# Opening the recurrence's buffers before layer 1's attention

## The chip, the cores and the metric

The kernel runs on one core of one Trainium2 chip. A core has five engines that work in parallel, each through its own list of instructions in order: TensorE (PE: matrix products, and transposes by a product with the identity), VectorE (DVE), ScalarE (ACT), GpSimd (POOL) and SyncE (SP, which here only issues DMAs). They wait for one another through semaphores. Data lies in SBUF (128 partitions), products in PSUM banks. The metric is the device time of one execution in microseconds. The kernel before the change takes 1873.88 us, the median of three runs (1872.47 to 1874.83).

## The reference

Two layers work on x, 3327 rows of 256 features, and on a symmetric 0/1 adjacency matrix. Layer 0 is a graph attention with two heads, followed by a mixture of 16 experts. Layer 1 is a graph attention with one head, followed by a recurrence of 30 steps on the normalized rows. The change lies in layer 1, where this is computed:

```python
# graph attention of layer 1, on h = layernorm(x)
wh = h @ W
e = wh @ a[:256] + (wh @ a[256:]).T
e = where(e > 0, e, 0.2 * e)
e = where(adj > 0, e, -9e15)
x = x + elu(softmax(e, axis=-1) @ wh)

# recurrence of layer 1, on h = layernorm(x); 30 times
h = h + 0.01 * tanh(h)
h = h * sigmoid(h)
h = layernorm(h, ln_w, ln_b)
h = h @ W.T + b

x = x + h
```

## The kernel before, in words

The rows are cut into 26 tiles of 128, which stay in SBUF as `x` the whole time. Everything is computed in float32.

Layer 1's attention (`attend`, L202) goes over nine parts of three target tiles each (`groups2`; the last part has two). In each part it goes over the 26 source tiles. For a source tile, ACT writes `e` (a Relu, L276), DVE makes the masked weights `pT` from `e`, the row `part` and the adjacency `adjT` (L281), and PE adds three products with `s_wh` to three accumulators in PSUM (L286; each product is two matmul instructions in the profile). `e` and `pT` have three buffers each (pool `edge2`). When a part is done, its accumulators are closed while the next part is already running: for each tile, DVE takes a reciprocal and the two halves of the elu from the accumulator (L257, L999, L1000), ACT an exponential (L1001), and DVE adds the result to `x` (L1002, L1003). `begin_state` (L1005) then stores the rows of `x` to DRAM as `kept` and normalizes them in place (statistics on DVE at L116 to L119, a power on POOL at L121, L128 on DVE). So `x` holds the recurrence's starting state, scaled by S = 100, for one part after another while the attention is still running.

The recurrence works on seven groups of four tiles (the last has two), 30 steps, so 210 groups in all, numbered through by `at`. A group goes through these steps, each a method of `Group`: `tanh` (ACT, L1046), `add` (POOL, L1049), `silu` (ACT, L1053), `measure` (DVE, L1058 and L1061), `invert` (POOL, L1066 and L1067), then a transposition of z, `product` (PE, L1101, with PSUM tile `po`) and `evict` (DVE, L1111, which writes the new `x`). The transposition has two forms. `turn_here` uses PE, eight transposes into two PSUM banks (L1077), and ACT copies these to `zT` (L1079). `turn_away`, for groups 1, 3 and 5 of every step, lets ACT split z into 16-bit halves (L1086), writes them to DRAM by a DMA of SP (L1087), and reads them back by a transposing DMA of SP (L1091). The loop at the end staggers the groups: in the pass `at`, the product of group `at` stands beside the tanh of group `at + 6` and the add of group `at + 5`.

A scheduler orders the instructions of each engine, from the dependencies and its own idea of durations; `tc.keep_in_program_order` takes an instruction out of its hands. The recurrence pins all its instructions from the second step on (`put`, L1041); in the first step it pins only PE's products and transposes.

Buffers come from pools. A pool that is opened after others were closed takes their memory, and its first writers wait for those that used it last. The names the change touches:

- `steps` (L944): two buffers each of `th`, `z` and `zT`, opened ahead of layer 1's attention. `add_results` (L956) uses them at the layer's start to load the experts' results (L962); in the recurrence `turn_here` takes its `zT`, and `turn_away` its `th` and `z`.
- `wide` (L1025): four buffers each of `wth` and `wz`, which hold the recurrence's tanh and silu. It is opened after the attention's pools (`keep2`, `work2`, `edge2`, `rows2`, `fin2`) are closed, and lies in their memory.
- `narrow` (L1026): the small statistics of the recurrence, opened at the same place.
- `ps` (two PSUM banks, opened ahead of the attention), `ps_t` and `ps_o`, opened after it. `turn_here` takes its banks from `ps` and `ps_t` in turn.

Of the kernel before, what the change touches and what calls it, by code (L numbers as in the profile page):

```python
# [11 lines left out]
F32 = mybir.dt.float32  # L12
I32 = mybir.dt.int32
I16 = mybir.dt.int16
# [7 lines left out]
P = 128  # L22
# [4 lines left out]
G = 4  # L27
# [4 lines left out]
def gat_moe_gat_recurrent_ffn(ctx: ExitStack, tc: tile.TileContext, a: dict, out: bass.AP):  # L32
    nc = tc.nc
    N, D = a["x"].shape
    KD = D // P
# [88 lines left out]
    def normalized(src, dst, scale=1.0):  # L124

        r, mv, power = inverse(src, scale)
        for j in range(len(src)):
            nc.vector.tensor_scalar(  # L128
                dst[j], src[j], mv[:, j, 0:1], r[:, j : j + 1], op0=ALU.subtract, op1=ALU.mult
            )  # L130
        return power

    def without_mean(wv, n_out, ones, p):

        for k in range(KD):
            nc.tensor.matmul(p[:, :n_out], lhsT=ones, rhs=wv[:, k, :], start=(k == 0), stop=(k == KD - 1))
        for k in range(KD):
            nc.vector.scalar_tensor_tensor(
                wv[:, k, :], p[:, :n_out], -1.0 / D, wv[:, k, :], op0=ALU.mult, op1=ALU.add
            )  # L140
# [43 lines left out]
    class Scores:  # L184


        def __init__(self, pool, heads, s=None):
            self.s = pool.tile([P, NT, 2, heads], F32, name="s") if s is None else s
            self.row = pool.tile([P, NT, heads], F32, name="row")
            self.full = pool.tile([P, NT, heads], F32, name="full")  # L190
            self.part = pool.tile([P, NT, heads], F32, name="part")
            self.minus = pool.tile([P, NT, heads], F32, name="minus")
# [189 lines left out]
    with ExitStack() as moe:  # L382
# [267 lines left out]
        two = rec.tile([P, 2, SLOTS], F32, name="prod")  # L650
# [290 lines left out]


    kept = dram.tile([NP, D], F32, name="kept")
    steps = ctx.enter_context(tc.tile_pool(name="steps", bufs=2))  # L944
    ps = ctx.enter_context(tc.tile_pool(name="ps2", bufs=2, space=PSUM))
    with ExitStack() as st:
        keep = st.enter_context(tc.tile_pool(name="keep2", bufs=1))

        s_wh = keep.tile([P, NT, 1, D + 3], F32, name="s_wh")
        wh = s_wh[:, :, :, 2:]  # L950
        sc = Scores(keep, 1, s_wh[:, :, 0, 0:2].rearrange("p t (s h) -> p t s h", h=1))
        work = st.enter_context(tc.tile_pool(name="work2", bufs=2))
        ps_o = st.enter_context(tc.tile_pool(name="ps2o", bufs=2, space=PSUM))
        names = cycle(("th", "z", "zT"))

        def add_results(some):  # L956
            for ts in some:
                n, two = len(ts), []
                for k in range(2):
                    here = slice(k * NP + ts[0] * P, k * NP + (ts[-1] + 1) * P)  # L960
                    two.append(steps.tile([P, G, D], F32, name=next(names))[:, :n, :])
                    nc.sync.dma_start(two[k], given[here, :].rearrange("(t p) d -> p t d", p=P))  # L962
                here = x[:, ts[0] : ts[-1] + 1, :]
                for k in range(2):
                    nc.vector.tensor_tensor(here, here, two[k], ALU.add)


        without_mean(wv1, D + 2, ones_r, ps.tile([P, 512], F32, name="bank"))
        recurrence_parameters(lambda: ps.tile([P, 512], F32, name="bank"))
        add_results(groups1[:3])  # L970
        tc.keep_in_program_order(nc.vector.memset(wh[:, :, :, D : D + 1], 1.0))
        count = 1

        def spot():
            nonlocal count
            count += 1
            return ps_o.tile([P, 512], F32, name=f"acc{count % 3}")

        def split1(t, p, r):
            nc.scalar.activation(s_wh[:, t, 0, : D + 2], p[:, : D + 2], AF.Copy, scale=r)  # L980
            for ts in groups1:
                if t == ts[-1]:
                    sc.finish(ts[0], t + 1)

        project(
            groups1, wv1, D + 2, split1, work, ps, spot,
            lambda ts, power: add_results(groups1[groups1.index(ts) + 3 :][:1]),
        )
        nc.vector.tensor_scalar(wh[:, NT - 1], wh[:, NT - 1], real[:, 0:1], None, op0=ALU.mult)

        run = st.enter_context(tc.tile_pool(name="edge2", bufs=3))
        rows_p = st.enter_context(tc.tile_pool(name="rows2", bufs=2))
        fin = st.enter_context(tc.tile_pool(name="fin2", bufs=2))

        def add_elu(t, pr, h, po, r):

            low = fin.tile([P, D], F32, name="low")
            high = fin.tile([P, D], F32, name="high")
            nc.vector.tensor_scalar(low[:pr], po, r, 0.0, op0=ALU.mult, op1=ALU.min)  # L999
            nc.vector.tensor_scalar(high[:pr], po, r, 0.0, op0=ALU.mult, op1=ALU.max)  # L1000
            nc.scalar.activation(low[:pr], low[:pr], AF.Exp)  # L1001
            nc.vector.scalar_tensor_tensor(high[:pr], low[:pr], -1.0, high[:pr], op0=ALU.add, op1=ALU.add)  # L1002
            nc.vector.tensor_tensor(x[:pr, t, :], x[:pr, t, :], high[:pr], ALU.add)  # L1003

        def begin_state(ts):  # L1005
            here = slice(ts[0] * P, (ts[-1] + 1) * P)
            nc.sync.dma_start(kept[here, :].rearrange("(t p) d -> p t d", p=P), x[:, ts[0] : ts[-1] + 1, :])
            yield
            tiles = [x[:, t, :] for t in ts]
            normalized(tiles, tiles, S)  # L1010

        attend(
            sc, wh, 1, groups2, 1, add_elu, begin_state, (run, rows_p, ps, ps_o), deque(),
            (nc.sync, 1, lambda: fin.tile([P, D], F32, name="low")),
        )


    with ExitStack() as st:
# [3 lines left out]
        last_p = st.enter_context(tc.tile_pool(name="last", bufs=2))  # L1022

        apart = [dram.tile([G * P, 2, D], I16, name=f"apart{q}") for q in range(2)]
        wide = st.enter_context(tc.tile_pool(name="wide", bufs=4))  # L1025
        narrow = st.enter_context(tc.tile_pool(name="narrow", bufs=8))  # L1026

        AWAY = (1, 3, 5)
        COUNT = len(groups)
        LAST = N_STEPS * COUNT  # L1030

        class Group:

            def __init__(self, at):
                self.at = at
                self.ts = groups[at % COUNT]
                self.n = len(self.ts)
                self.hs = x[:, self.ts[0] : self.ts[0] + self.n, :]
                self.away = at % COUNT in AWAY

            def put(self, ins):  # L1041
                return tc.keep_in_program_order(ins) if self.at >= COUNT else ins

            def tanh(self):
                self.th = wide.tile([P, G, D], F32, name="wth")[:, : self.n, :]
                self.put(nc.scalar.activation(self.th, self.hs, AF.Tanh, scale=1.0 / S))  # L1046

            def add(self):
                self.put(nc.gpsimd.tensor_tensor(self.th, self.th, self.hs, ALU.add))  # L1049

            def silu(self):
                self.z = wide.tile([P, G, D], F32, name="wz")[:, : self.n, :]
                self.put(nc.scalar.activation(self.z, self.th, AF.Silu, scale=1.0 / S))  # L1053

            def measure(self):
# [12 lines left out]

            def turn_here(self):
                pool = next(turns)  # L1070
                zT = steps.tile([P, G, KD, P], F32, name="zT")
                for c in range(self.n // 2):
                    pt = pool.tile([P, 2, KD, P], F32, name="bank")
                    for j in range(2):
                        for k in range(KD):
                            tc.keep_in_program_order(
                                nc.tensor.transpose(pt[:, j, k, :], self.z[:, 2 * c + j, k * P : (k + 1) * P], ident)  # L1077
                            )
                    self.put(nc.scalar.copy(zT[:, 2 * c : 2 * c + 2, :, :], pt))  # L1079
                self.zT = lambda j, k: zT[:, j, k, :]  # L1080

            def turn_away(self):
                n = self.n
                parts = steps.tile([P, G, 2, D], I16, name="th")[:, :n]
                here = apart[self.at % COUNT // 2 % 2][: n * P]
                self.put(nc.scalar.copy(parts, self.z.bitcast(I16).rearrange("p j (d b) -> p j b d", b=2)))  # L1086
                nc.sync.dma_start(  # L1087
                    here.rearrange("(j p) b d -> p j (b d)", p=P), parts.rearrange("p j b d -> p j (b d)")
                )
                zT = steps.tile([P, KD, G * P], F32, name="z")  # L1090
                nc.sync.dma_start(  # L1091
                    zT.bitcast(I16)[:, :, : n * 2 * P], here.rearrange("t b d -> (t b) d"), transpose=True
                )
                self.zT = lambda j, k: zT[:, k, j * P : (j + 1) * P]
# [98 lines left out]
```

## Time and profile before

| | |
|---|---|
| median of three runs | 1873.88 us (1872.47 to 1874.83) |
| the profiled execution: its time / its span | 1875.77 us / 1874.0 us |
| granted TensorE clock, mean of the span | 0.992 |
| PE busy | 1815.3 us, 97% of the span |
| DVE / ACT / POOL busy | 1281.8 / 1177.1 / 936.9 us |
| layer 1's attention, first to last product | 784.2 to 1080.9 us |
| first tanh of the recurrence | 1080.93 us |
| product of the second step's first group | 1124.74 us |
| one settled step | 25.5 us |

PE, DVE, ACT and POOL are named as above; SPq is SP's list of DMA issues, PEld the loading of weights, which runs beside PE. Times in the timeline count from the start of the span. In brackets stands how long the engine sat idle before an instruction and what ended that idle time. A number such as L1046 is a line of the kernel before; in the changed kernel the same line stands four or five lines further down.

### The profile page before, as it was taken

To read this page: it belongs to the slowest core of one execution; us is meant where nothing else is said; L and a number is where in the kernel's file an instruction comes from. 1 tells how busy PE (TensorE), PEld (TensorE's weight loads), DVE (VectorE), ACT (ScalarE), POOL (GpSimd) and SP (SyncE) were. 2 spreads that over 40 slices of the span, in tenths; PEclk is the share of its full clock that TensorE was granted. 3 is DMA by queue.
4 is the path that set the end of the run, shared out by engine and by line. 5 is a ranking of instruction groups with operands and counts; after the bars stand their busy time and mean duration, and the time that the engine had idled before them with its cause. 6 is when DMAs were issued, how large, how long until landed. Compare 5 with 4: busy or idle time off the path is not lost.

```text
span 1874.0 us, 32159 instructions
## 1 busy us (share of the span) xinstructions
PE 1815.3 (97%) x11204; PEld 1658.8 (89%) x11204; DVE 1281.8 (68%) x3829; ACT 1177.1 (63%) x1487; POOL 936.9 (50%) x864
## 2 busy tenths in 40 slices
PE   6999999999999998999999979999999999999997
PEld 6999999998999997788888868888888888888886
DVE  6888888842222222666767678888888888888887
ACT  2877777631111111655555578888888888888884
POOL 3010212255333331100000079999999999999994
PEclk9999999999999999999999989999999999999999
DMA  8887260179999885300000045545554555554556
GB/s 175 113 126 96 53 99 23 59 237 300 344 336 338 298 273 183 106 13 18 22 13 17 16 110 133 124 127 122 124 124 124 124 127 122 125 122 124 124 130 197
DMA packets 379919, 255.04 MB, mean 136 GB/s; under 512 B 240917, under 2 KB 339532, under 8 KB 379754
## 3 DMA queue, kind: packets, MB, share of 16 engines
q1 hardware_dynamic: 363634, 220.08, 43.0%
q0 software_dynamic: 11440, 28.09, 8.6%
q10 hardware_dynamic: 4680, 4.76, 0.8%
q8 instruction: 92, 1.51, 0.3%
q14 instruction: 73, 0.60, 0.1%
HBM read 168.19 MB, written 77.01 MB: 131 GB/s over the span
## 4 chain that ended last, share of the span: by engine, by line
PE 67%; issue 10%; POOL 6%; DVE 5%; DMA 4%; ACT 1%; SPq 0%; POOLq 0%; DVEq 0%; ACTq 0%
PE po L1101 34%; PE acc L286 25%; PE bank L1077 5%; POOL given L855 2%; POOL rb L761 2%; DVE pT L281 2%; DMA given<-wh,to 2%; DMA old<-kept 1%; DMA wh<-in_w_dram 1%; PE bank L835 1%; POOL wth L1049 1%; PE acc L163 1%; PE bank L526 1%; PE bank L148 0%; DMA lists<-pair,ati 0%
## 5 line engine op out<-in xcount | busy, mean ns | idle before, releaser
L276 ACT ACTIVATE e<-rb,minus,full 128x384 f32<-128x384 f32 (+3 forms) x494 | 402.4, 824 | 189.2 <-DVE pT L281 172.4
L1049 POOL TENSOR_TENSOR wth<-wth,x 128x1024 f32<-128x1024 f32 (+1 forms) x210 | 464.8, 2214 | 17.2 <-ACT wth L1046 17.2
L281 DVE SCALAR_TENSOR_TENSOR pT<-e,part,adjT 128x384 f32<-128x384 f32 (+3 forms) x494 | 374.7, 761 | 135.8 <-PE acc L286 120.4
L1111 DVE SCALAR_TENSOR_TENSOR x<-po,rr,bb 128x256 f32<-128x256 f32 x780 | 322.9, 475 | 99.4 <-PE po L1101 63.3
L1101 PE MATMUL po<-wc,zT 128*128 128x256 f32 x1680 | 384.2, 380 | 3.2 <-DVE x L1111 3.2
L1101 PEld LDWEIGHTS po<-wc,zT 128*128 128x128 f32 x1680 | 313.4, 191 | 43.1 <-ACT wz L1053 2.2
L1101 PE MATMUL po<-wc,z 128*128 128x256 f32 x1440 | 325.6, 379 | 0.0
L286 PE MATMUL acc<-wh,pT 128*128 128x129 f32 x2704 | 309.8, 276 | 2.1 <-DVE pT L281 2.1
L286 PEld LDWEIGHTS acc<-wh,pT 128*128 128x128 f32 x2704 | 305.0, 192 | 2.7 <-DVE pT L281 2.5
L1101 PEld LDWEIGHTS po<-wc,z 128*128 128x128 f32 x1440 | 271.3, 190 | 35.7
L286 PE MATMUL acc<-s_wh,pT 128*128 128x257 f32 x1352 | 295.8, 382 | 2.4 <-DVE pT L281 2.4
L286 PEld LDWEIGHTS acc<-s_wh,pT 128*128 128x128 f32 x1352 | 257.6, 191 | 40.4 <-DVE pT L281 3.8
L1058 DVE BATCH_NORM_STATS2 stats<-wz 128x6 f32<-128x256 f32 x780 | 274.4, 413 | 27.5 <-ACT wz L1053 27.3
L1053 ACT ACTIVATE wz<-wth 128x1024 f32<-128x1024 f32 (+1 forms) x210 | 208.0, 990 | 82.7 <-POOL wth L1049 82.4
L121 POOL TENSOR_TENSOR rstd<-ve,neg_half 128x4 f32<-128x4 f32 (+3 forms) x28 | 30.4, 1087 | 441.4 <-DVE ve L119 290.4
L1046 ACT ACTIVATE wth<-x 128x1024 f32<-128x1024 f32 (+1 forms) x210 | 209.8, 999 | 26.7 <-DVE x L1111 22.7
L1067 POOL TENSOR_TENSOR rr<-rr,neg_half 128x4 f32<-128x4 f32 (+1 forms) x210 | 208.2, 992 | 17.5
L1086 ACT COPY th<-wz 128x2048 int16<-128x2048 int16 x90 | 170.9, 1899 | 1.8
L881 ACT ACTIVATE e<-bank 128x512 f32<-128x512 f32 x61 | 36.4, 597 | 196.2 <-PE bank L835 188.8
L885 DVE TENSOR_TENSOR pT<-e,bank 128x512 f32<-128x512 f32 x61 | 41.9, 687 | 166.8 <-PE bank L835 166.7
L835 PEld LDWEIGHTS bank<-hT,wh 128*128 128x128 f32 x1280 | 149.3, 192 | 5.2 <-ACT hT L827 1.4
L835 PE MATMUL bank<-hT,wh 128*128 128x128 f32 x1280 | 150.5, 275 | 2.6 <-DMA wh<-in_w_dram 2.6
(195 smaller groups left out, 1636.3 us busy)
## 6 DMA issues: line engine op xcount, KB each, us to landing
wh<-in_w_dram SPq DMA_DIRECT2D x120, 512.0 KB
apart<-th SPq DMA_DIRECT2D x90, 512.0 KB
first_set<-in_w_dram SPq DMA_DIRECT2D x63, 512.0 KB
in_bytes<-in_adj_dram POOLq DMA_DIRECT2D x3, 2496.0 KB, 28.3
x<-in_x_dram SPq DMA_DIRECT2D x6, 512.0 KB
kept<-x SPq DMA_DIRECT2D x8, 384.0 KB
old<-kept SPq DMA_DIRECT2D x6, 512.0 KB
out_dram<-x SPq DMA_DIRECT2D x6, 512.0 KB
```

The lines of the kernel that those rows point to most:

```text
L276: nc.scalar.activation(e[:, : n * P], rb[:, : n * P], AF.Relu, scale=sc.full[:, j, h : h + 1], bias=sc.minus[:, j, h : h + 1],)
L281: masked = nc.vector.scalar_tensor_tensor(pT[:, : n * P], e[:, : n * P], sc.part[:, j, h : h + 1], adjT[:, j // 2, ts[0] * P : (ts[-1] + 1 ...
L286: nc.tensor.matmul(po[c], lhsT=pT[:, c * P : (c + 1) * P], rhs=wh[:, j, h, :], start=(j == 0 and c % per_bank == 0), stop=(j == NT - 1), s ...
L835: nc.tensor.matmul(p[:, f, :], lhsT=w[:, k, f * P : (f + 1) * P], rhs=hT[:, k, :], start=(k == 0), stop=(k == KD - 1),)
L1046: self.put(nc.scalar.activation(self.th, self.hs, AF.Tanh, scale=1.0 / S))
L1049: self.put(nc.gpsimd.tensor_tensor(self.th, self.th, self.hs, ALU.add))
L1053: self.put(nc.scalar.activation(self.z, self.th, AF.Silu, scale=1.0 / S))
L1058: self.put(nc.vector.bn_stats(stats[:, j, :], self.z[:, j, :]))
L1067: self.put(nc.gpsimd.tensor_tensor(r, r, neg_half[:, : self.n], ALU.pow))
L1086: self.put(nc.scalar.copy(parts, self.z.bitcast(I16).rearrange("p j (d b) -> p j b d", b=2)))
L1101: nc.tensor.matmul(self.po[:, j, :], lhsT=self.zT(j, k), rhs=wc[:, k, :], start=(k == 0), stop=(k == KD - 1),)
L1111: nc.vector.scalar_tensor_tensor(self.hs[:, j, :], self.po[:, j, :], self.r[:, j : j + 1], bb, op0=ALU.mult, op1=ALU.add)
```

## The change

The buffers of the recurrence's tanh and silu (now `th` with three buffers and `z` with four) move to the pools that are opened ahead of layer 1's attention, and so do the statistics (`narrow`). `add_results` uses the same pools as before, now with 3, 4 and 2 buffers. `turn_away` gets a pool of its own, `apart`, opened where `wide` was. In the first step, group 1 is turned by PE instead of through DRAM (`and at > 1`), and the transposes of groups 0 and 1 are no longer pinned.

```diff
-    steps = ctx.enter_context(tc.tile_pool(name="steps", bufs=2))
+    steps = {
+        name: ctx.enter_context(tc.tile_pool(name=f"steps_{name}", bufs=bufs))
+        for name, bufs in (("th", 3), ("z", 4), ("zT", 2))
+    }
+    narrow = ctx.enter_context(tc.tile_pool(name="narrow", bufs=8))
...
-                    two.append(steps.tile([P, G, D], F32, name=next(names))[:, :n, :])
+                    name = next(names)
+                    two.append(steps[name].tile([P, G, D], F32, name=name)[:, :n, :])
...
-        wide = st.enter_context(tc.tile_pool(name="wide", bufs=4))
-        narrow = st.enter_context(tc.tile_pool(name="narrow", bufs=8))
+        apart_p = st.enter_context(tc.tile_pool(name="apart", bufs=2))
...
-                self.away = at % COUNT in AWAY
+                self.away = at % COUNT in AWAY and at > 1
...
-                self.th = wide.tile([P, G, D], F32, name="wth")[:, : self.n, :]
+                self.th = steps["th"].tile([P, G, D], F32, name="th")[:, : self.n, :]
...
-                self.z = wide.tile([P, G, D], F32, name="wz")[:, : self.n, :]
+                self.z = steps["z"].tile([P, G, D], F32, name="z")[:, : self.n, :]
...
-                zT = steps.tile([P, G, KD, P], F32, name="zT")
+                zT = steps["zT"].tile([P, G, KD, P], F32, name="zT")
...
-                            tc.keep_in_program_order(
+                            (tc.keep_in_program_order if self.at > 1 else lambda ins: ins)(
...
-                parts = steps.tile([P, G, 2, D], I16, name="th")[:, :n]
+                parts = apart_p.tile([P, G, 2, D], I16, name="parts")[:, :n]
...
-                zT = steps.tile([P, KD, G * P], F32, name="z")
+                zT = apart_p.tile([P, KD, G * P], F32, name="zTa")
```

## The prediction

> **What bounds the kernel now.** I read the page first: the chain that ended last is 67% PE, and its largest line, L1101 (the recurrence's products), fills the whole second half. Then the table of busy time by stage (columns: stretch, its length, then busy time and instruction count of PE, PEld, DVE, ACT and POOL, granted clock, DMA share, GB/s):
>
> ```profile
> 784.20:1055.30 271.10, 271.10 (x1243) 237.22 (x1244) 172.25 (x383) 153.91 (x231) 5.96 (x7) 0.99 0.05 17
> 1055.30:1080.90 25.60, 24.63 (x111) 20.30 (x109) 18.47 (x52) 14.12 (x25) 0.95 (x1) 1.00 0.05 16
> 1080.90:1124.70 43.80, 31.26 (x148) 27.09 (x148) 35.68 (x117) 35.65 (x40) 37.55 (x33) 0.84 0.45 119
> 1150.50:1176.00 25.50, 25.50 (x133) 22.62 (x133) 21.18 (x79) 22.90 (x26) 24.57 (x22) 1.00 0.52 129
> ```
>
> Layer 1's attention (784 to 1081) and a settled step (1150 to 1176) keep PE busy all the time. Only the joint is loose: 43.80 us with PE at 31.26 and at 0.84 of its clock. What PE does there, from the timeline, is 104 product matmuls and 44 transposes; in a settled step they take 0.216 and 0.130 us, so 22.5 + 5.7 = 28.2 us of work. The joint loses 15.6 us. The timeline of the joint shows to what (start, length, engine, instruction, idle time before it):
>
> ```profile
> 1080.93 1.06 ACT L1046 ACTIVATE wth<-x 128x1024 f32<-128x1024 f32 x1 [4.01 <-PE acc L286]
> 1082.06 4.84 POOL L1049 TENSOR_TENSOR wth<-wth,x 128x1024 f32<-128x1024 f32 x2 [16.33 <-ACT wth L1046]
> 1082.48 2.21 DVE L1002 SCALAR_TENSOR_TENSOR high<-low,high 128x256 f32<-128x256 f32 x1
> 1083.56 1.28 ACT L1053 ACT_TABLE_LOAD   x1
> 1084.72 2.47 DVE L1003 TENSOR_TENSOR x<-x,high 128x256 f32<-128x256 f32 x1
> 1084.86 1.06 ACT L1053 ACTIVATE wz<-wth 128x1024 f32<-128x1024 f32 x1
> 1085.97 1.97 PE L1077 MATMUL bank<-ident,wz 128*128 128x128 f32 x8 [5.08 <-ACT wz L1053]
> 1088.85 1.88 ACT L1086 COPY th<-wz 128x2048 int16<-128x2048 int16 x1
> 1090.75 0.38 SPq L1087 DMA_DIRECT2D apart<-th  x1
> 1093.73 2.25 SPq L1091 DMA_TRANSPOSE z<-apart  x1
> 1095.39 5.24 PE L1101 MATMUL po<-wc,zT 128*128 128x256 f32 x16
> 1100.46 3.62 PE L1101 MATMUL po<-wc,z 128*128 128x256 f32 x16
> ```
>
> The first tanh waited 4.01 us for PE's last attention matmul: its inputs were done long before, but its buffer was attention's memory. Then tanh, add, silu run one after another while PE waits, and group 1 goes through DRAM: copy end 1090.7 to its product at 1100.5, 9.7 us. Last, the attention, where the first step is to be moved:
>
> ```profile
> 979.73 50.45 PE L286 MATMUL acc<-s_wh,pT 128*128 128x257 f32 x232
> ...
> 996.82 0.58 DVE L281 SCALAR_TENSOR_TENSOR pT<-e,part,adjT 128x384 f32<-128x384 f32 x1
> ...
> 1002.11 0.62 DVE L281 SCALAR_TENSOR_TENSOR pT<-e,part,adjT 128x384 f32<-128x384 f32 x1 [0.68 <-PE acc L286]
> 1002.76 0.71 ACT L276 ACTIVATE e<-rb,minus,full 128x384 f32<-128x384 f32 x1 [0.59 <-DVE pT L281]
> ```
>
> PE runs 232 matmuls without a gap, one source tile (six of them) in 1.30 us; DVE idles 0.68 and ACT 0.59 of each 1.30, both waiting for buffers. With three pT buffers a pT is begun some 2.3 us before PE needs it and ends 1.7 us before (2.60 - 0.62, less about 0.3 of hand-over; single records agree). At its tightest, behind the closing of the part before (the pT at 996.82), only 0.5 us is left.
>
> **What the Trainium skill says.** "SBUF — State Buffer", section "SBUF: two separate sides": DVE and GpSimd share a port pair as an exclusive lock; a DVE operation with two SBUF inputs and a GpSimd operation reading SBUF block each other for a whole instruction. The trace agrees: L1002 and L1003, 0.41 us in the attention, took 2.21 and 2.47 while two adds of 2.4 us ran on POOL, each ending just after one. L281 reads e and adjT, both in SBUF. "ScalarE: Activation LUTs", section "What ACT_TABLE_LOAD costs", has 1283 ns plus a drain of about 1380; here the load took 1.28 and silu began 0.02 after it, so I take 1.28. "TensorE: Matmul & The Clock Gate", Part 1, says an idle PE drops to half clock: sixteen matmuls took 5.24 at 1095.39 and 3.62 at 1100.46.
>
> **The change part by part.** The instruction order of the two builds says where things go.
>
> *Buffers.* th and z now lie in pools opened before the attention. The changed order puts tanh, add, silu and stats of groups 0, 1, 2, 3 into parts 3, 4, 5, 7 of the attention's nine, group 4's tanh and add into part 8, its silu and group 5's tanh and add into the last; group 0's eight transposes and two zT copies too. th falls from 4 buffers to 3: tanh then waits for the silu three groups back, which stands before it on ACT; nothing. The settled step's order is the same on every engine, so I cost it at nothing; PE's 25.5 us of work covers it (POOL's 24.57 is the nearest rival). The loads of `given` at L962 get more buffers; DVE's additions behind them stand back to back, in the same order: nothing, at most 1 us either way.
>
> *Joint after the change*, from PE's last attention matmul (0). DVE reads the last two acc tiles till 1.65 (in the trace 1080.9 to 1082.56), PE waits. Then transposes of groups 1 and 2 (2 x 1.04) to 3.7, product 0 (16 x 0.216 = 3.46) to 7.2, product 1 to 10.7, transposes 4, products 2 and 3 to 18.6, transposes 6 (0.5), product 4 to 22.6, transposes 7, products 5 and 6 (1.7) to 28.9, transposes 9; step 2's first product at 29.9. ACT's order: copy for group 3 (1.9), Exp load 1.28, two exps 0.8, two zT copies of group 1 to 5.1 (needed 7.2), Silu load, silu 5, its copy, zT copies of group 2 to 10.4 (needed 11.7). DVE: evict 0 waits behind a statistic of group 5 (7.5 to 7.9) and L128, ends 10.2 (product 2 needs its po buffer at 11.7). On SP, group 3's write is issued at 1.9, its transpose stands behind the last `kept` store, whose x is done at about 5.3: landed 6.7 later, 12, needed 15.2. So PE is fed throughout. Before, the same stretch took 1080.89 to 1124.74 = 43.85: gain 13.9, group 1's eight added transposes (1.04) included; the 9.7 us path through DRAM is gone for it.
>
> *Attention after the change.* (a) Group 0's transposes: 1.0 us of PE. (b) Each add holds the lock 2.37 us. A pT about to begin ends up to 2.37 late against 1.7 of slack; the add follows a tanh that starts behind an e, so it takes the lock shortly before the next pT: 0.5 us lost, five times, 2.5. Ends: 0 if L281 is not blocked, 0.9 each if two pT are caught. Silu itself holds ACT back by tanh 1.06 + load 1.28 + wait for the add + 1.06, some 2.7 us behind its turn, under the 3 to 4 us by which e runs ahead: nothing. (c) Four closings get an Exp load: exp and so x come late, the pT behind x's statistics by 0.6 against 0.5 of slack: 0.15 x 4 = 0.6 (0 to 2). (d) In the last part a source tile takes 0.87 us, and pT's slack is 1.0. ACT, busy 14.1 us there, gets 1.06 (zT) + 1.28 + 1.06 + 1.06 more. Counted from the part's first matmul, the zT copies end near 7.1, behind group 0's transposes; two e, then the load to 9.6 and silu 4 to 10.7. DVE stands at a statistic of it, then three L128 (1.06) and the pT: 12.6, where PE wants it at 11.3: 1.35 lost. Then group 5's add makes a pT 2.2 late, against 1.0: 1.2 lost. Together 2.6 (1 to 5). Sum 1.0 + 2.5 + 0.6 + 2.6 = 6.7.
>
> Net 13.9 - 6.7 = 7.2. The profiled execution had a span of 1874.0 (1875.8 as timed), the runs a median of 1873.88: 1866.7. The tail (DMA of `old`) moves along unchanged.
>
> **Rivals.** (1) Attention's slack hides nearly all: L281 not blocked, closings free: only 1.0 + 1.0 is paid, gain 11.9, 1862. For it: PE was never short of a pT in 271 us. Against: L1002 and L1003. (2) Attention takes nearly all: 0.9 x 5 + 2 + 5 + 1.0 = 12.5, gain 1.4, 1872.5. For it: 0.5 us of slack in closings, and the last part already loses 1 us of PE. (3) Slower, by table switches. The order has eleven loads where there was one, and ACT takes them in line. If each costs the page's 2.66 and not 1.28, 1.4 more stands ahead of the exps that DVE waits for with the pT behind it: 4 x 1.4 in the closings; about 0.7 at each of four silus, which then pass the lead of e; 1.4 in the last part; 1.5 in the joint, where two loads eat the 1.3 that zT of group 2 has to spare: 11.3 on top of 6.7, so 1878. It turns the sign from 2.2 us a switch on (7.2 / 11.3 x 1.4 + 1.28). Against it stands the 0.02 us between load and silu. (4) That the change does not act can be left aside: the first tanh stands behind the sixteenth e of part 3, and needs no attention memory.
>
> **How the numbers follow.** About 0.2% (3.75 us) is what this measurement can tell from no change. Forecast 0.60, own range 1864 to 1870; rival 1 0.20; rival 2 0.13; rival 3 0.07. Faster by over 0.2% (below 1870.1): nearly all of the forecast and rival 1, 0.78. Same: the forecast's edge and most of 2: 0.16. Slower: rival 3, most of it, 0.06. Range 1861.5 to 1872.5: out of it fall rival 3, half of 2 and the fast edge of 1.
>
> **What would show it.** A first tanh near the middle of part 3; PE's step from the last acc matmul to step 2's first product near 30 us, clock near 1.0; pT of 2 to 3 us beside each add, PE gaps of about 0.5 there; the last part some 3.5 us longer. Wrong it would be if attention's 296.7 us grew by far more or less than 6.7, if load and silu stood further apart, or if PE in the joint waited for a zT of group 1, 2 or 3.

## The result, and the profile after

The changed kernel took 1862.68 us, the median of six runs (1862.0 to 1863.88), against 1875.09 us (1872.47 to 1877.23, six runs) for the kernel before on the same chip: a ratio of 0.9936, with a 95% interval of 0.9923 to 0.9949. That is 12.4 us less, where 7.2 were forecast. The profiled executions have spans of 1860.3 and 1874.0 us, 13.7 apart.

The table of busy time by stage, of the changed kernel, with the columns of the one in the prediction (stretch, length, then busy time and instructions of PE, PEld, DVE, ACT and POOL, granted clock, DMA share, GB/s). The stretches are, nearly, the first eight parts of the attention, the last part, the joint (from the attention's last product to the second step's first), and a later step:

```profile
785.30:1057.00 271.70, 271.31 (x1249) 236.92 (x1250) 186.84 (x419) 171.63 (x249) 24.43 (x20) 1.00 0.05 17
1057.00:1083.30 26.30, 24.64 (x113) 20.02 (x111) 20.22 (x57) 17.35 (x31) 4.88 (x4) 1.00 0.05 16
1083.30:1112.40 29.10, 27.33 (x149) 24.48 (x150) 22.82 (x79) 26.00 (x29) 18.62 (x17) 1.00 0.57 153
1112.40:1138.00 25.60, 25.60 (x135) 22.72 (x134) 21.28 (x79) 22.66 (x26) 24.39 (x22) 1.00 0.52 126
```

The joint fell from 43.80 to 29.10 us, its clock rose from 0.84 to 1.00, and PE lacks only 1.8 us of being busy throughout. POOL's and ACT's work of the first step now stands in the attention (POOL 5.96 to 24.43 us, ACT 153.91 to 171.63), and PE is still busy for 271.31 of 271.70 us there.

The joint itself, from the timeline of the changed kernel (start, length, engine, instruction, idle time before it):

```profile
1083.29 1.90 ACT L1090 COPY parts<-z 128x2048 int16<-128x2048 int16 x1 [4.01 <-PE acc L286]
1085.07 1.94 PE L1081 MATMUL bank<-ident,z 128*128 128x128 f32 x16 [1.81 <-DVE high L1005]
1085.21 1.28 ACT L1006 ACT_TABLE_LOAD   x1
1086.84 7.07 PE L1105 MATMUL po<-wc,zT 128*128 128x256 f32 x32
1090.04 2.06 SPq L1095 DMA_TRANSPOSE zTa<-apart  x1
1094.63 3.62 PE L1105 MATMUL po<-wc,zT 128*128 128x256 f32 x16
1098.08 3.62 PE L1105 MATMUL po<-wc,zTa 128*128 128x256 f32 x16
1112.36 1.89 PE L1105 MATMUL po<-wc,zT 128*128 128x256 f32 x8
```

PE waits once, 1.81 us for DVE to read the last accumulators. Then groups 1 and 2 are turned (1085.07), products 0 and 1 run back to back at full speed (1086.84), product 2 follows at 1094.63, and group 3's data, through DRAM, is there when product 3 wants it at 1098.08. The second step begins at 1112.36 (the line counts the first eight matmuls of its product). The 4.01 us of waiting for PE's last attention product, which stood before the first tanh, now stands before the copy of group 3 into `parts`, whose pool `apart` still takes over the attention's memory.

### Where the 13.7 us are

From the same trace, and from those of the runs below, I took the length of each stretch of the attention (first product of a part to first product of the next) and of the joint. The joint is measured here from the start of the attention's last matmul to step 2's first product, 0.4 more than in the prediction (43.85 there is 44.23 here). Each ratio is to the kernel before on the same chip.

| kernel | ratio to before, 95% | part 3 | part 4 | part 5 | part 7 | last part | joint |
|---|---|---|---|---|---|---|---|
| before | 1 | 33.81 | 33.81 | 33.81 | 33.81 | 24.05 | 44.23 |
| the change | 0.9936 (0.9923 to 0.9949) | 34.31 | 33.91 | 33.81 | 34.22 | 25.95 | 29.48 |
| first transposes pinned | 0.9929 (0.9917 to 0.9942) | 34.31 | 33.91 | 33.81 | 34.21 | 25.39 | 29.96 |
| group 1 through DRAM | 0.9977 (0.9971 to 0.9983) | 34.31 | 33.91 | 33.81 | 34.23 | 25.95 | 36.50 |
| pinned from group 4 on | 0.9938 (0.9925 to 0.9951) | 34.30 | 33.91 | 33.81 | 34.22 | 26.21 | 29.48 |
| buffers in attention's memory | 1.0007 (0.9999 to 1.0015) | 33.81 | 33.81 | 33.81 | 33.81 | 24.05 | 45.53 |
| first step without addition | 0.9932 (0.9918 to 0.9945) | 33.81 | 33.81 | 33.81 | 33.81 | 25.15 | 29.48 |
| first step without silu's table | 0.9928 (0.9915 to 0.9942) | 34.32 | 34.27 | 34.26 | 34.23 | 25.07 | 29.48 |
| additions in quarters | 0.9931 (0.9917 to 0.9944) | 33.81 | 34.23 | 33.96 | 33.81 | 25.15 | 29.48 |
| group 4 after the attention | 0.9932 (0.9919 to 0.9946) | 33.81 | 33.90 | 33.81 | 33.81 | 24.05 | 31.01 |
| the same, group 5's addition in quarters | 0.9928 (0.9914 to 0.9942) | 33.81 | 33.91 | 33.81 | 33.81 | 24.05 | 30.48 |

Parts 2, 6 and 8 took 33.81 in all of them. The joint gained 14.75 us; the attention lost 0.50 + 0.10 + 0.41 + 1.90 = 2.91; the other 28 steps gained 0.08. That is 11.9. The remaining 1.8 of the span lie ahead of part 2 (819.8 to 819.2) and in the tail (34.8 to 33.6), and are not the change's: in three profiles of the changed kernel the first of these was 819.2, 822.2 and 823.7 and the tail 33.6, 33.9 and 34.1. Part 1 alone took 35.60 before and 33.92 in the change, at a granted clock of 0.79 and 1.00 from 784 to 792 us; but 35.60 stands again in three kernels that contain the change (pinned from group 4 on, without addition, additions in quarters). The columns of the table, on the other hand, repeat to 0.02 us.

### The profile page after: what moved, and what is told of

Same layout as the page of the kernel before. It is cut to its first block, busy times and chain, and to the rows that moved or that the text cites. A ratio compares the mean times of both kernels' runs of the same rounds, so it can differ in the third digit from the quotient of the medians.

```text
span 1860.3 us, 32198 instructions
## 1 busy us (share of the span) xinstructions
PE 1809.2 (97%) x11212; PEld 1653.9 (89%) x11212; DVE 1284.7 (69%) x3829; ACT 1186.9 (64%) x1498; POOL 939.3 (50%) x864
## 4 chain that ended last, share of the span: by engine, by line
PE 67%; issue 10%; DVE 6%; POOL 5%; DMA 5%; ACT 0%; SPq 0%; POOLq 0%; DVEq 0%; ACTq 0%
PE po L1105 35%; PE acc L286 24%; PE bank L1081 5%; DVE pT L281 3%; POOL given L855 2%; POOL rb L761 2%; DMA given<-wh,to 2%; DMA wh<-in_w_dram 1%; DMA old<-kept 1%; DMA lists<-pair,ati 1%; PE bank L835 1%; PE acc L163 1%; PE bank L526 1%; POOL rstd L121 1%; PE bank L148 0%
## 5 line engine op out<-in xcount | busy, mean ns | idle before, releaser
L1053 POOL TENSOR_TENSOR th<-th,x 128x1024 f32<-128x1024 f32 (+1 forms) x210 | 465.1, 2215 | 16.0 <-ACT th L1050 14.4
L281 DVE SCALAR_TENSOR_TENSOR pT<-e,part,adjT 128x384 f32<-128x384 f32 (+3 forms) x494 | 383.3, 780 | 118.8 <-PE acc L286 103.4
L1105 PE MATMUL po<-wc,zTa 128*128 128x256 f32 x1424 | 321.9, 379 | 0.0
L1105 PEld LDWEIGHTS po<-wc,zTa 128*128 128x128 f32 x1424 | 268.3, 190 | 35.3
L1062 DVE BATCH_NORM_STATS2 stats<-z 128x6 f32<-128x256 f32 x780 | 275.1, 413 | 20.7 <-ACT z L1057 20.6
L1057 ACT ACTIVATE z<-th 128x1024 f32<-128x1024 f32 (+1 forms) x210 | 207.9, 990 | 76.9 <-POOL th L1053 76.7
L1050 ACT ACTIVATE th<-x 128x1024 f32<-128x1024 f32 (+1 forms) x210 | 209.8, 1000 | 27.0 <-DVE x L1115 24.1
L1090 ACT COPY parts<-z 128x2048 int16<-128x2048 int16 x89 | 169.1, 1900 | 5.9 <-PE acc L286 4.0
```

Source lines behind the costliest of these rows:

```text
L281: masked = nc.vector.scalar_tensor_tensor(pT[:, : n * P], e[:, : n * P], sc.part[:, j, h : h + 1], adjT[:, j // 2, ts[0] * P : (ts[-1] + 1 ...
L1062: self.put(nc.vector.bn_stats(stats[:, j, :], self.z[:, j, :]))
L1105: nc.tensor.matmul(self.po[:, j, :], lhsT=self.zT(j, k), rhs=wc[:, k, :], start=(k == 0), stop=(k == KD - 1),)
```

## The experiments

**The change again.** The changed kernel ran twice more, each time beside other kernels of the table.

> The changed kernel unaltered, as the measure for the others of this call. If the 1.1 us later start of the attention and the 1.2 us shorter tail seen in its first trace belong to the change, they are there again; if they are the weather of one execution, they are not. Time 12.4 us under the kernel before, give or take 1.5.

> The change itself, as a measure of the same call for the run beside it: joint 29.48, last part 25.95, stretches of 34.31, 33.91 and 34.22, ratio to before near 0.9936.

Measured: ratios of 0.9936 both times (0.9923 to 0.9949, and 0.9922 to 0.9949); 29.48 in the joint and 25.95 and 25.96 in the last part. The gain holds.

**Group 1 through DRAM, with the early buffers.**

```diff
-                self.away = at % COUNT in AWAY and at > 1
+                self.away = at % COUNT in AWAY
```

> Undoes one part alone: group 1 of the first step goes through DRAM again, with the early buffers kept. My theory (the early buffers carry the gain; the DRAM path costs only what product 0 does not cover): copy to 1.9 us after the attention, its transpose behind group 3's write on SP to 6.3, landed at 13.0; PE has product 0 done at 6.2 and waits 6.8, less 0.95 of transposes saved: 5 to 6 us slower than the changed kernel, so 6 to 7 under the kernel before. Rival (taking group 1 off the DRAM path is the main part of the gain): 9 to 12 us slower than the changed kernel.

Measured: 0.9977, joint 36.50, 7.0 longer. The timeline of this run:

```profile
1087.25 1.90 ACT L1090 COPY parts<-z 128x2048 int16<-128x2048 int16 x1 [4.01 <-PE acc L286]
1093.93 4.96 SPq L1095 DMA_TRANSPOSE zTa<-apart  x2
1099.63 5.27 PE L1105 MATMUL po<-wc,zTa 128*128 128x256 f32 x16 [6.08 <-ACT th L1050]
```

Group 1's z was finished long before, but its way through DRAM begins with `parts`, which waits for the attention's memory; from the end of that copy (1089.15) to product 1 it is 10.5 us, and PE has only product 0 to cover them. It idles 6.08 us, and then runs product 1 at a low clock (0.70 granted on the mean from 1099.6 to 1104.9), 5.27 instead of 3.62: this 1.65 is what the expectation left out. (The profile names ACT as what ended the wait; of what product 1 needs, the transposing DMA is the last that the trace shows.)

**The buffers back in the attention's memory, group 1 still turned by PE.**

```diff
-        for name, bufs in (("th", 3), ("z", 4), ("zT", 2))
+        for name, bufs in (("th", 2), ("z", 2), ("zT", 2))
...
+        late = {
+            name: st.enter_context(tc.tile_pool(name=f"late_{name}", bufs=bufs)) for name, bufs in (("th", 3), ("z", 4))
+        }
...
-                self.th = steps["th"].tile([P, G, D], F32, name="th")[:, : self.n, :]
+                self.th = late["th"].tile([P, G, D], F32, name="th")[:, : self.n, :]
...
-                self.z = steps["z"].tile([P, G, D], F32, name="z")[:, : self.n, :]
+                self.z = late["z"].tile([P, G, D], F32, name="z")[:, : self.n, :]
```

> As the change, but th and z of the recurrence come from pools opened after the attention, in its memory (the pools ahead of it keep two buffers each, which only the start of the layer uses). Group 1 is still turned by PE. Theory: it is the memory that holds the first step back, so no tanh starts before PE's last attention matmul, tanh, add, silu and transposes of group 0 run one after another while PE waits, and step 2's first product comes about 42 us after the last attention matmul: the 29.5 of the change, 10.7 for the product of group 0 that comes 14.5 instead of 3.8 us after it, and 1.6 for sixteen products at the low clock. Attention's last part falls to 24.05, the stalls of 0.5 and 0.4 in the parts go. Sum 12.3 - 2.9 = about 9.5 us slower than the change, 2 to 3 us faster than the kernel before. Rival, the scheduler's order and the unpinned transposes carry it, not the memory: joint 29.5, no difference from the change. Second rival, gains of the two parts add up (7.7 for the buffers, 7.0 for group 1, as turning group 1 away again showed): joint 37 us, 4 to 5 us slower than the change.

Measured: 1.0007, no gain left. The attention is as before to 0.01 us in every part from the second on, and the joint, 45.53, is even 1.3 longer, where about 42 was expected. Its timeline (lines of this kernel: tanh L1053, addition L1056, silu L1060, transposes L1084):

```profile
1081.26 1.06 ACT L1053 ACTIVATE th<-x 128x1024 f32<-128x1024 f32 x1 [4.01 <-PE acc L286]
1082.39 7.31 POOL L1056 TENSOR_TENSOR th<-th,x 128x1024 f32<-128x1024 f32 x3 [16.33 <-ACT th L1053]
1085.06 2.45 DVE L1008 TENSOR_TENSOR x<-x,high 128x256 f32<-128x256 f32 x1
1090.54 1.28 ACT L1060 ACT_TABLE_LOAD   x1 [5.72 <-DVE x L1008]
1092.95 4.45 PE L1084 MATMUL bank<-ident,z 128*128 128x128 f32 x24 [11.72 <-ACT z L1060]
1097.24 7.07 PE L1108 MATMUL po<-wc,zT 128*128 128x256 f32 x32
1110.90 3.72 PE L1108 MATMUL po<-wc,zTa 128*128 128x256 f32 x16 [2.26 <-DVE x L1118]
```

So the early memory is what the gain needs: with nothing moved but th and z, the first tanh falls back to the first moment after PE's last attention product. Three additions in a row then hold DVE's closings, silu's table load waits 5.72 us for the last of these (L1008), and PE waits 11.72 us. This second wait is one more that memory makes, and the kernel before did not have it: there the load at 1083.56 and the silu behind it waited for no closing. Group 0's silu needs no data of those closings; but by the two memory plans, the pool of z here reaches over the `low` and `high` buffers of the closings (`fin2`), which `wide` left free. Products 0 and 1 do run together (1097.24), as they do in the change, but the groups behind them come late, and PE waits another 2.26 us at product 3: what group 1 saved there is lost again. With this run and the one above, the parts of the change don't add: early buffers alone gain 7.7 us of the joint, group 1 on PE with late buffers gains nothing, both gain 14.75. What group 1 on PE would give with th and z exactly where they lay before was not tried; the 1.3 lost here contain the wait for L1008.

**First transposes pinned again.**

```diff
-                            (tc.keep_in_program_order if self.at > 1 else lambda ins: ins)(
+                            tc.keep_in_program_order(
```

> Undoes one part alone: the first step's transposes are pinned again. Group 0's transposes then stand behind the attention, and group 4's silu with them, since its z buffer comes free only by them. My theory (the transposes were free where they stood, in PE's waits at a closing, but the silu they let in cost the last part 1.0 us of its 1.9): the last part gets back 1.0 us, the joint pays 0.9 for the transposes; within 1 us of the changed kernel. Rival (having the transposes and zT ready is what keeps the joint short): the joint grows by 3 us or more, to over 32 us.

Measured: 0.9929 beside the change's 0.9936 on the same chip, which is no difference; by the stretches it is 0.56 less in the last part and 0.48 more in the joint. The last part gave back less than the 1.0 expected: the loss behind silu 4 went with it, but group 5's addition now began within 0.02 us of a pT and cost 1.34 instead of 0.80. Where group 0's eight transposes stand hardly matters, and the reason shows in the last part of the changed kernel:

```profile
1061.48 0.93 PE L1081 MATMUL bank<-ident,z 128*128 128x128 f32 x7
1062.36 2.00 PE L286 MATMUL acc<-s_wh,pT 128*128 128x257 f32 x8
```

and at the same place in the kernel before:

```profile
1061.90 2.00 PE L286 MATMUL acc<-s_wh,pT 128*128 128x257 f32 x8 [0.71 <-DVE pT L281]
```

The transposes filled a wait that PE had there anyway, behind the closing of part 8. The products of the fourth to ninth source tiles follow one another in the same periods in both kernels, to 0.01 us (0.99, 1.85, 0.97, 1.28, 0.97). The last two runs below confirm it: with these transposes and their copies as the only work of the first step there, the last part takes 24.05, as before.

**The first step without its addition.** This kernel leaves out `h + 0.01 tanh(h)`'s sum in the first step.

```diff
-                self.put(nc.gpsimd.tensor_tensor(self.th, self.th, self.hs, ALU.add))
+                if self.at >= COUNT:
+                    self.put(nc.gpsimd.tensor_tensor(self.th, self.th, self.hs, ALU.add))
```

> As the change, but the first step leaves out the addition of x to its tanh (seven additions on POOL), so it computes something else in that step. Theory, the lock between POOL's addition and DVE's L281 makes all of PE's stalls in the parts: the third, fourth and seventh stretch (34.31, 33.91, 34.22 us) go back to 33.81, the last part loses the 0.7 us at its thirteenth source tile and keeps the 1.0 at its tenth: about 25.2. Joint unchanged at 29.5. In all 1.7 us less. Rival, ACT's extra work (tanh, load of the table, silu) makes the stalls: the parts stay at 34.31, 33.91 and 34.22, the last at 25.9, no difference.

Measured as the theory had it: parts 3, 4 and 7 back to 33.81, the last part at 25.15, joint the same. So POOL's addition makes all of PE's loss in the parts, and 0.8 of the last part's 1.9; the table loads, which this kernel keeps, cost the parts nothing by themselves. What an addition costs depends on its phase, that is, on when the next pT's turn comes while it runs. The two ways in which it can fall are in the timeline of the changed kernel. Part 3, where PE lost 0.50:

```profile
864.32 4.43 DVE L281 SCALAR_TENSOR_TENSOR pT<-e,part,adjT 128x384 f32<-128x384 f32 x4
864.92 2.35 POOL L1053 TENSOR_TENSOR th<-th,x 128x1024 f32<-128x1024 f32 x1 [1.61 <-PE acc L286]
867.75 7.42 PE L286 MATMUL acc<-s_wh,pT 128*128 128x257 f32 x33 [0.23 <-DVE pT L281]
```

and part 5, where it lost nothing:

```profile
933.77 2.35 POOL L1053 TENSOR_TENSOR th<-th,x 128x1024 f32<-128x1024 f32 x1 [2.26 <-ACT th L1050]
934.54 2.52 DVE L281 SCALAR_TENSOR_TENSOR pT<-e,part,adjT 128x384 f32<-128x384 f32 x2 [0.68 <-PE acc L286]
934.91 1.28 ACT L1057 ACT_TABLE_LOAD   x1
936.21 1.06 ACT L1057 ACTIVATE z<-th 128x1024 f32<-128x1024 f32 x1
```

In part 3 the first of the four pT ends just as the addition begins, so the second is held for nearly all of its 2.35 us, more than the 1.7 that it runs ahead of PE. In part 5 the addition had run 0.77 us when the next pT's turn came: it is held for 1.58 us, until 936.12, and that the 1.7 cover.

**The first step without silu's table.** A second tanh stands in place of the silu in the first step, so the tables need not be changed there.

```diff
-                self.put(nc.scalar.activation(self.z, self.th, AF.Silu, scale=1.0 / S))
+                self.put(nc.scalar.activation(self.z, self.th, AF.Silu if self.at >= COUNT else AF.Tanh, scale=1.0 / S))
```

> As the change, but the first step takes a second tanh in place of the silu, so that ACT loads no table for it in the attention and the joint; it computes something else in that step. Theory: the loads cost PE nothing in the parts, which stay at 34.31, 33.91 and 34.22; in the last part the silu ends 1.28 us earlier, and the 1.0 us lost at the tenth source tile goes, 24.9 to 25.2 in all; joint 29.5 or up to 0.3 less. About 1 us less than the change. Rival, the loads make the stalls of the parts too: all of them back at 33.81, the last part near 24.7, 2.2 us less.

Measured: 0.9928, last part 25.07 and joint 29.48, as the theory had it for these. Against the rival, no part got shorter. But parts 4 and 5 took 34.27 and 34.26, 0.4 more than with the table loads, which neither the theory nor the rival had foreseen. The lines of part 4:

```profile
900.90 1.95 DVE L281 SCALAR_TENSOR_TENSOR pT<-e,part,adjT 128x384 f32<-128x384 f32 x1 [0.68 <-PE acc L286]
903.56 0.76 DVE L1062 BATCH_NORM_STATS2 stats<-z 128x6 f32<-128x256 f32 x2 [0.71 <-ACT z L1057]
```

It is not the lock that grew: the pT beside the addition takes 1.95 here, and 2.27 and 1.99 in parts 4 and 5 of the change. What differs is DVE's order. In the change the first statistic of silu stands behind the fourteenth pT of the part, here behind the thirteenth; DVE waits there for the silu, 0.71 us (0.17 and 0.23 in the change), and the fourteenth pT is late. That the order alone makes the difference is read from the trace, not tried.

**Additions in quarters.**

```diff
-                self.put(nc.gpsimd.tensor_tensor(self.th, self.th, self.hs, ALU.add))
+                if self.at >= COUNT:
+                    self.put(nc.gpsimd.tensor_tensor(self.th, self.th, self.hs, ALU.add))
+                    return
+                for j in range(self.n):
+                    nc.gpsimd.tensor_tensor(self.th[:, j, :], self.th[:, j, :], self.hs[:, j, :], ALU.add)
```

> As the change, with each addition of the first step cut into four of a quarter of the width (128x256). Theory: each of them holds DVE's L281 up for at most its own length, some 0.6 us (a quarter of 2.36), which the 1.7 us by which pT runs ahead cover; PE's stalls from the additions go as if the additions were gone: third, fourth and seventh stretch at 33.81, the last part near 25.2, joint 29.5, 1.7 us less than the change. Rival, four in a row shut DVE out as one of 2.4 us does: 34.31, 33.91, 34.22 and 25.9, no difference.

Measured: parts 3 and 7 at 33.81 and the last part at 25.15, as if the additions were gone; but part 4 lost 0.42 and part 5 0.15. DVE gets in between the quarters, so no pT is held for long; the four together, however, take longer than one whole, and in part 4 the silu waits for them and DVE for the silu (timeline of this kernel, where the addition is L1057, silu L1061, its statistics L1066; the first line has the last three of the four quarters, the first of which began at 902.97):

```profile
903.74 2.72 POOL L1057 TENSOR_TENSOR th<-th,x 128x256 f32<-128x256 f32 x3
906.49 1.06 ACT L1061 ACTIVATE z<-th 128x1024 f32<-128x1024 f32 x1 [1.10 <-POOL th L1057]
907.58 0.43 DVE L1066 BATCH_NORM_STATS2 stats<-z 128x6 f32<-128x256 f32 x1 [1.70 <-ACT z L1061]
```

DVE idles 1.70 us at a statistic with pT behind it. Cutting takes away most of the lock and feeds this other wait; in all it saves 1.2 us of the attention's 2.9, too little for the time to show.

**Pinned from group 4 on.**

```diff
-                return tc.keep_in_program_order(ins) if self.at >= COUNT else ins
+                return tc.keep_in_program_order(ins) if self.at >= 4 else ins
```

> One change more: the pinning starts at group 4 of the first step, not at step 2. Groups 0 to 3 stay early; group 4's silu and group 5's tanh and add move behind the attention, and with them an Exp and a Silu table load. My theory (the last part lost 1.9 us to the statistic that waits for silu 4 and to add 5's lock; ACT has the room behind the attention): the last part gets back 1.5 to 1.9, the joint stays at 29 to 30 us; 1 to 2 us faster than the changed kernel. Rival (groups 4 and 5 were needed early): PE waits in the joint for zT of group 2 or z of group 4, the joint grows by 2 us or more, no gain.

The expectation for the last part fell: 26.21 where about 24 was expected, and 0.9938, no better than the change. The pins took silu 4 and group 5 out of the last part, and the scheduler put group 4's tanh and addition there instead. The timeline:

```profile
1070.36 2.60 POOL L1053 TENSOR_TENSOR th<-th,x 128x1024 f32<-128x1024 f32 x1 [31.74 <-DVE ve L119]
1071.11 2.12 DVE L281 SCALAR_TENSOR_TENSOR pT<-e,part,adjT 128x256 f32<-128x256 f32 x1 [0.37 <-PE acc L286]
1072.91 1.04 POOL L121 TENSOR_TENSOR rstd<-ve,neg_half 128x3 f32<-128x3 f32 x1
1073.99 1.06 DVE L128 TENSOR_SCALAR x<-x,mv,rstd 128x256 f32<-128x256 f32 x3 [0.75 <-POOL rstd L121]
```

One addition holds a pT for some 1.6 us where a source tile takes 0.87, and the closing's power on POOL waits behind it, DVE behind the power, three pT behind DVE: PE's periods there are 1.58 and 2.21 us, 2.1 lost. The joint stays at 29.48 although nothing of silu 4, tanh 5 and addition 5 is done ahead of it: groups 0 to 3, with group 4's tanh and addition, are early enough. The next two runs make those of group 4 late as well.

**Group 4 kept out of the attention.** Made from the last two: group 4's tanh of the first step gets a buffer of a pool opened after the attention, everything from group 4 on is pinned, and the additions of groups 0, 3 and 4 are cut.

```diff
+        late = st.enter_context(tc.tile_pool(name="late", bufs=1))
...
-                self.th = steps["th"].tile([P, G, D], F32, name="th")[:, : self.n, :]
+                pool, name = (late, "th4") if self.at == 4 else (steps["th"], "th")
+                self.th = pool.tile([P, G, D], F32, name=name)[:, : self.n, :]
...
-                return tc.keep_in_program_order(ins) if self.at >= COUNT else ins
+                return tc.keep_in_program_order(ins) if self.at >= 4 else ins
...
-                self.put(nc.gpsimd.tensor_tensor(self.th, self.th, self.hs, ALU.add))
+                if self.at not in (0, 3, 4):
+                    self.put(nc.gpsimd.tensor_tensor(self.th, self.th, self.hs, ALU.add))
+                    return
+                for j in range(self.n):
+                    nc.gpsimd.tensor_tensor(self.th[:, j, :], self.th[:, j, :], self.hs[:, j, :], ALU.add)
```

> As the change, with group 4 of the first step kept out of the attention: its tanh gets a buffer of a pool that is opened after the attention, in the attention's memory, and groups 4, 5 and 6 of the first step are pinned. The additions of groups 0, 3 and 4 are cut into four. Theory: the last part keeps only group 0's transposes and copies, which fall into a wait that the kernel before has too: 24.1 us instead of 25.95. The third and seventh stretch go to 33.81, the fourth stays at 33.91. The joint stays at 29.5, since 3 us stood between group 3's landing and its use, of which its copy now loses 1.06 to the tanh ahead of it. In all 2.8 us less than the change. Rival: group 4's additions now hold DVE's closings of the last two tiles up, x of them and so the last store of kept and the transposing DMA behind it on SP come some 2 us later, and PE waits for group 3: joint 31 to 32, no gain over the change or one below 1 us.

Measured: the attention is 2.8 us shorter, as expected, but the joint 1.53 longer, near the rival's size, and not by the rival's transfer: product 3 follows product 2 without a wait. The timeline of this run (addition L1056, eviction L1121, products L1111):

```profile
1091.39 2.36 POOL L1056 TENSOR_TENSOR th<-th,x 128x1024 f32<-128x1024 f32 x1
1092.10 2.13 DVE L128 TENSOR_SCALAR x<-x,mv,rstd 128x256 f32<-128x256 f32 x2 [1.46 <-DMA kept<-x]
1095.75 1.62 DVE L1121 SCALAR_TENSOR_TENSOR x<-po,rr,bb 128x256 f32<-128x256 f32 x4
1097.51 3.69 PE L1111 MATMUL po<-wc,zT 128*128 128x256 f32 x16 [1.30 <-DVE x L1121]
```

Group 0's eviction, at 1091.56 in the change (8.3 us after the end of the last attention product), comes 11.1 us after it here, and product 2 waits 1.30 us for it. The last run takes group 5's addition (1091.39) apart as well, the lock on L128 being one candidate:

```diff
-                if self.at not in (0, 3, 4):
+                if self.at not in (0, 3, 4, 5):
```

> As the run with group 4 kept out of the attention, with group 5's addition of the first step cut into four too. In that run the attention gave 2.8 us back and the joint took 1.5 more: group 5's whole addition (2.36 us) held DVE's L128 of the last tile up, the eviction of group 0 came behind it, and PE waited 1.30 us for it ahead of product 2. Theory: with quarters L128 takes its own 0.7, the eviction comes 1.5 us earlier, PE's wait is gone and the joint is 29.5 to 29.9; attention 294.74 as there; 2.4 to 2.8 us less than the change, ratio to before about 0.992. Rival, the place of group 4 in the joint is the cause (its silu and statistics stand ahead of the eviction), not the lock: joint stays at 31.

Measured: joint 30.48, PE's wait ahead of product 2 at 0.76. So cutting this addition gave back a third, 0.53 of 1.53. The eviction still comes 10.5 us after the last attention product: L128 takes 1.64 us beside the quarters (0.72 in the change), and group 4's statistics stand between it and the eviction. How the rest divides between these two was not tried. By the stretches this version gains 2.82 - 1.00 = 1.8 us on the change; the ratio, 0.9928 (0.9914 to 0.9942), can't be told from 0.9936.

## Why the prediction was right, and where it was off

**The joint.** Right in its mechanism and nearly in its size: 43.85 to 29.9 was forecast, 43.85 to 29.10 came. PE's wait (1.65 forecast, 1.81 measured), product 0 at 3.7 (3.6), product 1's end at 10.7 (10.7) and product 3 at 15.2 (14.8) stood where the sum had them; the 0.8 is transposes that run a little into the products beside them (eight were counted as 1.04 us; from 1093.75 to the product at 1094.63 they take 0.88). PE was fed throughout, group 3's transfer included. That the first tanh waited for memory and not for data, which the step *buffers* rested on, is shown by the run with the old memory, where that tanh waits for PE's last attention product again, and which lost the whole gain. The rival in which the change doesn't act is out: the first tanh runs at 863.79, in part 3. (It stands behind the thirteenth e of that part, not the sixteenth, as the text had it.)

**Attention, the terms that were mis-sized.** 6.7 us were forecast, 2.9 paid.
- (a), group 0's transposes, 1.0: nothing. They fell into PE's wait behind a closing, which the lines of the kernel before show; the runs with group 4 kept out, where they stand in a last part of 24.05, confirm it. The term counted work on a busy engine without asking whether its engine was waiting just there.
- (b), the addition's lock, 0.5 in each of five parts, 2.5: 1.0 in all (0.50, 0.10, 0, 0.41, 0). The lock is as "SBUF — State Buffer" in the Trainium skill has it ("SBUF: two separate sides"): in part 5 above, the pT begun at 934.54, while an addition ran until 936.12, took 1.99 us instead of 0.6. The worst case of 0.5 is right; but it needs a pT whose turn comes with the addition's start, and that held in two parts of five.
- (c), closings behind an Exp load, 0.6: nothing. Parts 4, 5, 6 and 8, whose closing begins with the load, lost at most 0.10, and that went with the addition while the loads stayed. (By the term's own figures, 0.6 of delay against 0.5 of slack, it was 0.1 a closing and not 0.15.)
- (d), the last part, 2.6: 1.9, in the two steps foreseen. Their lines in the changed kernel:

```profile
1066.47 0.43 DVE L1062 BATCH_NORM_STATS2 stats<-z 128x6 f32<-128x256 f32 x1 [0.99 <-ACT z L1057]
1068.31 2.87 PE L286 MATMUL acc<-s_wh,pT 128*128 128x257 f32 x12 [0.83 <-DVE pT L281]
1069.02 2.36 POOL L1053 TENSOR_TENSOR th<-th,x 128x1024 f32<-128x1024 f32 x1 [2.83 <-ACT th L1050]
1069.62 2.04 DVE L281 SCALAR_TENSOR_TENSOR pT<-e,part,adjT 128x256 f32<-128x256 f32 x1
1071.71 11.54 PE L286 MATMUL acc<-s_wh,pT 128*128 128x257 f32 x52 [0.54 <-DVE pT L281]
```

DVE waits 0.99 us at the statistic of silu 4 and then has three L128 ahead of the pT, which puts PE 1.09 us behind by the starts of its products (1.35 forecast); group 5's addition then holds a pT, 0.80 (1.2 forecast). The runs without the addition and without the table take away the second and the first, one each.

**The rivals.** The time came out at that of the first, "attention's slack hides nearly all" (1862), but its mechanism is half true: L281 was blocked, and it was the phase and the lead of pT that hid most of it. Attention taking nearly all is out by 9.6 us (12.5 against 2.9). The table switches, the slower side, are out: between load and silu stand 0.02 us in part 5 (934.91 + 1.28 to 936.21), so the drain in "What ACT_TABLE_LOAD costs" of "ScalarE: Activation LUTs" in the Trainium skill was not paid here; the step, that the switch costs its 1.28 us of ACT and no more, held, and the parts are at 33.81 in the run without the addition, which keeps the loads.

**The sum.** Of the span's 13.7 us against 7.2, 3.8 is attention over-priced, 0.8 the joint, 0.1 the other steps, and 1.8 the start and the tail, which vary between executions of one kernel. The measured 1862.68 lies below the forecast's own range of 1864 to 1870 and inside the wide one of 1861.5 to 1872.5: the mechanism of the joint was foreseen, the size of the attention's terms was not.

## What to carry to other kernels

A first instruction that waits for the last reader in a finished stage, while its data is ready, points to memory: opening its buffers ahead of that stage lets the next stage's head run under it, but every buffer on the way must move, since one that is left behind (`parts`) waits as the first did. Before a lock or an added instruction is priced at its full length on a busy engine, look where its start falls against the consumer's turn and against waits that are there already: here that made 2.9 us of 6.7. And when two edits shorten one chain, price them together: the early buffers gained 7.7 without the other, group 1 on PE gained nothing with late buffers, both gained 14.75. A pool that is moved back for a test may lie over other buffers than it did before, and wait for other readers: look at its waits before the run is taken for the old state.

## What the runs showed that was not expected

- Four additions of a quarter of the width free DVE between them, but from the start of the first to the end of the last they took 3.39 to 3.67 us on POOL in the attention, where one whole addition takes 2.35 to 2.63.
- Taking the table loads away made two parts of the attention 0.4 us longer: the silu's statistics moved up by one pT in DVE's order, and DVE waited for the silu with that pT behind it.
- Sixteen products after 6.08 us without work for PE took 5.27 us instead of 3.62, so a wait of 6.1 us cost 7.7.
- The lengths of the attention's later parts, the joint and the steps repeat to some 0.02 us between executions, while what lies ahead of them varied by 5 us (819.2 to 824.5): differences of half a microsecond can be read from stretches of a profile that the whole time will not show.
